# A four-layer kernel whose engine queues are ordered on another timing model

## The chip, the cores and the metric

The kernel runs on one core of a Trainium2 chip. The core has five engines that work side by side, each through its own queue, strictly in the order in which the program holds its instructions: TensorE (PE, matrix products; its weight loads are listed as PEld), VectorE (DVE), ScalarE (ACT), GpSimd (POOL) and SyncE (SP, which here only issues DMAs). An instruction that needs another engine's result waits on a semaphore, and everything behind it in its own queue waits with it.

The metric is device time in microseconds (us). Before the change the median of 3 runs is 3192.32 us (3189.55 to 3193.76).

## The reference, cut to what matters

Four batches of 1024 tokens with 128 channels go through four layers. Every layer has the same frame, with a different mixer and a different feed-forward part:

```python
xn = _layernorm(x)
s = mixer(xn)          # four kinds
g = silu(ffn(xn))      # four kinds
x = x + s * g
```

- Layer 0: a state-space mixer in chunks, and a gated feed-forward whose weights and inputs are rounded to a 4-bit grid.
- Layer 1: attention between the 16 heads of one token with 1.5-entmax (it sorts 16 scores for each head and token), and a mixture of 8 experts, of which each token uses two.
- Layer 2: a rotating linear recurrence over the tokens (16 heads, each with a 2 x 16 state), and a second mixture of experts with a shared expert.
- Layer 3: causal attention with a learned relative position term, 16 heads of 8 channels, and a gated feed-forward with 384 hidden units.

In layer 3 the part that the prediction speaks of most is

```python
srel = srel_skew(einsum('bhnd,hmd->bhnm', qx, ex))
qk = (einsum('bhnd,bhmd->bhnm', qx, kx) + srel) * inv_dim
atten = softmax(qk - mask)            # exp on ScalarE
h = silu(x @ wg.T) * (x @ wu.T)       # silu on ScalarE
```

## The kernel before, in words

The kernel is written in Python over a tile library. The code emits instructions one after another (generators are woven together by `weave`, L78 and following, so that the emitted order already mixes independent work). It doesn't say in which order an engine runs them. When the library's `TileContext` (L2228) is left, a scheduler plays the whole program through on a timing model. Whenever an engine is free in that model, it gets the earliest emitted instruction of those whose operands and buffers the model holds to be ready. The sequence that comes out is the fixed queue of each engine on the chip. So the timing model never sets a time on the chip, but it decides which instruction stands before which.

**Layer 1** works in eight units of half a batch (512 tokens). `heads1` computes a unit's head scores (products L718, sums L722), sorts them with a network of maxima and minima (`sort16`, L696 and L697, on DVE), runs two prefix scans (L750, L751) and the threshold search (L759 to L773), and forms the values (products on POOL at L788, sums on DVE at L783). `moe1` computes the router's logits (L803), ranks them (`top2`, L191 to L199), normalises the two weights (L809 to L816), splits them into three bf16 parts (`thirds`, L207 to L211) and turns these on PE (L214). Only then can the experts start: each expert scales its input (L830 on DVE), multiplies (L835 and L837 on PE), applies silu (L838 on ACT), multiplies on DVE (L839) and projects down (L826).

**Layer 2** first projects (L1100 to L1191), then computes rotation gates (`gates2`), then runs `scan2`: 8 tiles of 16 steps; a step is four dependent small DVE instructions (L1530, L1533, L1536, L1541). The steps read tables that `chunks2` makes (sums at L1396, updates at L1408 and L1409 on DVE; much of the rest on POOL). A table goes through DRAM: L1412 stores it and L1501 and L1502 load it again in the layout that the steps read. There are four tables, and tile i needs table i modulo 4. The experts of this layer (`experts2`) are emitted between the steps.

**Layer 3** handles 128 units (4 batches, 4 groups of heads, 8 query tiles), which makes 192 score tiles of up to 512 columns:

- PE computes a score tile for 4 heads (L2068) into the only `score` buffer there is (the PSUM pool `"sc"` has one buffer, so score tile x+1 waits until tile x has been compared);
- DVE scales, adds the relative term and takes the minimum (L2076, L2083);
- ACT takes the exponential (L2090), DVE transposes the result (L1797), PE multiplies it with the values (L2104);
- for later units, PE computes relative scores (L2004), ACT copies them out (L2006), DMAs store them and load them back skewed (L2009, L2010, L2025, L2031), POOL masks them (L2035).

Once per batch `ffn3` is emitted into this stream in four steps of three column blocks: PE L1953, then on ACT a silu (L1957) and a copy (L1958), a product on POOL (L1959), the down projection on PE (L1963) and another silu on ACT (L1964). ACT holds one table of functions at a time; going from exp to silu or back costs an `ACT_TABLE_LOAD`, which the compiler puts in after the order is fixed. Copies need no table of their own.

## Time and profile before

The profiled execution took 3191.88 us; its span in the profile is 3190.2 us. By stage (busy time of an engine in each stretch, in us):

| stage | from, to | length | PE | DVE | ACT | granted PE clock |
|---|---|---|---|---|---|---|
| layer 0 | 40, 578 | 538 | 401.74 | 284.90 | 270.92 | 0.87 |
| layer 1 | 578, 1278 | 700 | 513.12 | 563.95 | 244.74 | 0.80 |
| layer 2, projections | 1278, 1440 | 162 | 143.59 | 100.75 | 68.47 | 0.95 |
| layer 2, gates and scan | 1440, 2053 | 613 | 289.62 | 470.06 | 240.85 | 0.59 |
| layer 2, end | 2053, 2140 | 87 | 62.41 | 51.74 | 30.29 | 0.69 |
| layer 3 | 2140, 3190 | 1050 | 824.21 | 813.42 | 635.09 | 0.76 |

A row like `L2090 ACT ACT_TABLE_LOAD x17 | 21.8, 1283 | 0.3` is to be read as: source line, engine, operation, count; busy us, mean ns of one; idle us of the engine just before these instructions.

### The profile page before, as it was taken

To read this page: it belongs to the slowest core of one execution; us is meant where nothing else is said; L and a number is where in the kernel's file an instruction comes from. 1 tells how busy PE (TensorE), PEld (TensorE's weight loads), DVE (VectorE), ACT (ScalarE), POOL (GpSimd) and SP (SyncE) were. 2 spreads that over 40 slices of the span, in tenths; PEclk is the share of its full clock that TensorE was granted. 3 is DMA by queue.
4 is the path that set the end of the run, shared out by engine and by line. 5 is a ranking of instruction groups with operands and counts; after the bars stand their busy time and mean duration, and the time that the engine had idled before them with its cause. 6 is when DMAs were issued, how large, how long until landed. Compare 5 with 4: busy or idle time off the path is not lost. (4 is left out here: it accounts for less than half of the span.)

```text
span 3190.2 us, 50621 instructions
## 1 busy us (share of the span) xinstructions
PE 2246.5 (70%) x18321; PEld 1278.9 (40%) x18321; DVE 2302.6 (72%) x5540; ACT 1494.7 (47%) x3256; POOL 1155.6 (36%) x1086
## 2 busy tenths in 40 slices
PE   5787778577787776894443674367877877878875
PEld 2555556232333332561110222244544544545553
DVE  5555544878888886657777888656788788788786
ACT  3554544333333333525332463136665765665663
POOL 3433444144444444223477433232322322323322
PEclk9888888588878877895655566566877877877776
DMA  3000000100000000320333446328677677677772
GB/s 81 13 1 1 1 1 1 35 0 0 0 0 7 6 1 7 114 98 20 73 106 112 128 107 145 101 90 252 179 217 213 191 215 230 185 221 203 209 233 65
DMA packets 397311, 308.18 MB, mean 97 GB/s; under 512 B 96369, under 2 KB 379885, under 8 KB 391429
## 3 DMA queue, kind: packets, MB, share of 16 engines
q1 hardware_dynamic: 395908, 300.75, 32.9%
q10 hardware_dynamic: 1152, 4.19, 0.4%
q8 instruction: 144, 2.36, 0.3%
q14 instruction: 107, 0.87, 0.1%
HBM read 162.72 MB, written 141.56 MB: 95 GB/s over the span
## 5 line engine op out<-in xcount | busy, mean ns | idle before, releaser
L2090 ACT ACTIVATE neg<-neg,low 128x640 f32<-128x640 f32 (+7 forms) x512 | 390.1, 763 | 168.4 <-DVE low L2083 168.1
L2035 POOL TENSOR_SCALAR_AFFINE_SELECT rel<-rel 128x512 f32<-128x512 f32 x288 | 180.2, 637 | 625.6 <-DMA rel<-flat 459.6
L1797 DVE STREAM_TRANSPOSE wT<-neg 128x640 f32<-128x640 f32 (+7 forms) x512 | 361.7, 754 | 15.8 <-ACT neg L2090 13.4
L2068 PE MATMUL score<-k,q 32*128 32x512 f32 (+3 forms) x1536 | 276.5, 702 | 103.1 <-DVE low L2083 102.5
L2083 DVE CUSTOM_DVE_ANT_0 neg<-score,rel,low 128x128 f32<-128x128 f32 (+3 forms) x448 | 217.3, 517 | 138.2 <-issue 67.2
L2004 PE MATMUL pr<-emb,q 32*128 32x256 f32 x1024 | 227.5, 525 | 62.2 <-ACT r L2006 37.1
L2104 PE MATMUL po<-wT,vb 128*32 128x64 f32 (+1 forms) x10240 | 216.6, 241 | 44.4 <-issue 30.8
L2104 PEld LDWEIGHTS po<-wT,vb 128*32 128x32 f32 x10240 | 184.3, 128 | 144.1 <-issue 85.2
L2004 PEld LDWEIGHTS pr<-emb,q 32*128 32x128 f32 x1024 | 146.1, 249 | 136.9 <-ACT r L2006 69.1
L2006 ACT COPY r<-pr 128x512 f32<-128x512 f32 x256 | 136.4, 581 | 128.8 <-PE pr L2004 95.3
L2068 PEld LDWEIGHTS score<-k,q 32*128 32x128 f32 x1536 | 98.5, 236 | 159.8 <-DVE low L2083 115.5
L2083 DVE CUSTOM_DVE_ANT_0 neg<-score,rel 128x512 f32<-128x512 f32 (+3 forms) x320 | 149.2, 521 | 18.4 <-PE score L2068 7.2
L835 PE MATMUL pg<-xnT,w 128*128 128x512 f32 x256 | 148.1, 662 | 6.7 <-DVE h L839 3.1
L788 POOL TENSOR_TENSOR prod<-rest,kv 128x2048 f32<-128x2048 f32 x32 | 145.2, 4571 | 18.4 <-ACT rest L778 18.4
L837 PE MATMUL pu<-xin,w 128*128 128x512 f32 x256 | 141.2, 635 | 13.7 <-DVE h L839 7.6
L826 PE MATMUL po<-h,w 128*128 128x512 f32 x256 | 131.4, 635 | 26.9 <-DVE h L839 26.9
L838 ACT ACTIVATE h<-pg 128x512 f32<-128x512 f32 x128 | 75.9, 595 | 156.8 <-PE pg L835 156.7
L214 PE MATMUL pt<-ident,three 128*24 128x128 bf16 x64 | 9.2, 295 | 197.5 <-DVE three L211 197.5
L1084 PE MATMUL ph<-xin,upT 128*128 128x512 bf16 (+1 forms) x128 | 69.7, 574 | 65.2 <-DVE xin L1078 63.8
L431 PE MATMUL px<-hT,xbcT 128*128 128x512 f32 x256 | 114.7, 592 | 0.0
L1489 PE MATMUL read<-kt,const_sb 128*128 128x128 f32 x256 | 50.7, 370 | 90.3 <-POOL kt L1484 90.3
L783 DVE TENSOR_REDUCE s<-prod 128x128 f32<-128x2048 f32 x32 | 73.1, 2284 | 49.4 <-POOL prod L788 49.4
(634 smaller groups left out, 5662.8 us busy)
## 6 DMA issues: line engine op xcount, KB each, us to landing
flat<-r SPq DMA_DIRECT2D x256, 256.0 KB
rel<-flat SPq DMA_DIRECT2D x112, 512.0 KB
flat<-r SPq DMA_DIRECT2D x256, 128.0 KB
rel<-flat SPq DMA_DIRECT2D x96, 256.0 KB
kt<-kd SPq DMA_DIRECT2D x16, 512.0 KB
qt<-qd SPq DMA_DIRECT2D x16, 512.0 KB
kdc<-kdd SPq DMA_DIRECT2D x16, 512.0 KB
ktc<-ktd SPq DMA_DIRECT2D x16, 512.0 KB
```

Source lines behind the costliest of these rows:

```text
L788: nc.gpsimd.tensor_tensor(prod, attn.rearrange("p (t h g) -> p t h g", t=4, g=16)[:, t].unsqueeze(2).to_broadcast(each), kv[:, t, 1, :].re ...
L826: nc.tensor.matmul(po, W["w2"][:, e, c, :], h[:, c, :], start=(e == 0 and c == 0), stop=(e == 7 and c == 1))
L835: nc.tensor.matmul(pg, W["w1"][:, e, c * P : (c + 1) * P], xnT, start=True, stop=True)
L837: nc.tensor.matmul(pu, W["w3"][:, e, c * P : (c + 1) * P], xin, start=True, stop=True)
L1797: nc.vector.transpose(weights[at, pair][j][:, t % 2, 0 : (t + 1) * P], S[j][:, 0 : (t + 1) * P])
L2004: nc.tensor.matmul(to[:, m, :], q[at, t * P : (t + 1) * P], W["emb"][at, i, :], start=True, stop=True)
L2006: nc.scalar.copy(r[:, n], to)
L2035: nc.gpsimd.affine_select(out=rel[:, :, slot(back), :], in_=rel[:, :, slot(0), :], compare_op=op, fill=fill, base=0, pattern=[[0, 4], [-si ...
L2068: nc.tensor.matmul(sc[:, j, 0 : last - first], q[at(j), 1 + t * P : 1 + n], kk[at(j), first:last], start=True, stop=True)
L2083: nc.vector.tensor_tensor_reduce(out=neg[:, begin:last], in0=sc[:, j, begin - first : last - first], in1=rel[:, j, slot : slot + (last - b ...
L2090: nc.scalar.activation(neg[:, 0:n], neg[:, 0:n], AF.Exp, bias=here, scale=-1.0, accum_out=group["sums"][:, j, t : t + 1])
L2104: nc.tensor.matmul(o[32 * j : 32 * j + 32, 2 * pair + m.start : 2 * pair + 2, :], vb[:, kb, j].rearrange("p a d -> p (a d)"), weights[j][: ...
```

## The change

One argument is added where the library's context is opened. No instruction that computes is added, removed or resized.

```diff
     out = nc.dram_tensor("out_0", (NB, T, D), F32, kind="ExternalOutput").ap()
-    with tile.TileContext(nc) as tc:
+    with tile.TileContext(nc, schedule_with_timeline_sim=True) as tc:
         tile_kernel(tc, I, out)
```

With it, the scheduler plays the program through on the library's timeline model (engines, queues and DMAs as timelines) instead of its default model. All five queues are ordered anew, and what the compiler derives from the order (table loads, waits that need an instruction of their own) follows. On the new queues of DVE, ACT, PE, POOL and SP stand the same computing instructions as before, in another order.

## The prediction, made before the changed kernel had run

> **What bounds the kernel now.** I read the page's busy lines first, then the busy time by stage, then the waits of the two stages that are longest, and last ScalarE's timeline in layer 3. No engine is busy for more than 72% of the span, so no engine's work bounds the whole; each stage is bound by how tightly two queues mesh, and that is the one thing that this change can alter.
>
> ```profile
> span 3190.2 us, 50621 instructions
> ...
> PE 2246.5 (70%) x18321; PEld 1278.9 (40%) x18321; DVE 2302.6 (72%) x5540; ACT 1494.7 (47%) x3256; POOL 1155.6 (36%) x1086
> ```
>
> Busy time by stage (stretch, length, then PE, PEld, DVE, ACT, POOL, granted clock, DMA share, GB/s). These rows are layer 1, layer 2's projections, its gates and scan, and layer 3:
>
> ```profile
> 578.00:1278.00 700.00, 513.12 (x1156) 208.79 (x1156) 563.95 (x779) 244.74 (x459) 280.24 (x116) 0.80 0.02 6
> 1278.00:1440.00 162.00, 143.59 (x768) 99.81 (x768) 100.75 (x300) 68.47 (x145) 35.27 (x32) 0.95 0.31 104
> 1440.00:2053.00 613.00, 289.62 (x840) 117.55 (x840) 470.06 (x888) 240.85 (x476) 286.05 (x202) 0.59 0.36 93
> 2140.00:3190.00 1050.00, 824.21 (x13376) 519.27 (x13376) 813.42 (x2560) 635.09 (x1492) 304.56 (x412) 0.76 0.69 201
> ```
>
> Layer 1 and the scan are led by DVE (81% and 77% busy), layer 3 by PE and DVE together (78% and 77%). The waits of layer 1 and of layer 3 (total, times, longest):
>
> ```profile
> PE pt L214 <- DVE three L211: 108.3, 8, 16.2
> ...
> DVE s L783 <- POOL prod L788: 49.4, 28, 3.6
> ```
>
> ```profile
> ACT neg L2090 <- DVE low L2083: 168.1, 68, 8.5
> ...
> PE score L2068 <- DVE low L2083: 102.5, 88, 5.4
> ...
> DVE neg L2083 <- PE score L2068: 55.9, 47, 3.9
> ```
>
> In layer 1 PE stands idle about 13.5 us in each of 8 units until DVE has split the router's weights. In layer 3 PE and DVE take turns on the one score buffer. ScalarE's lines in layer 3, and one stretch of it inside a feed-forward:
>
> ```profile
> L2090 ACT ACT_TABLE_LOAD x17 | 21.8, 1283 | 0.3
> L1957 ACT ACT_TABLE_LOAD x9 | 11.5, 1283 | 4.4 <-issue 4.3
> ```
>
> ```profile
> 2483.86 1.28 ACT L1957 ACT_TABLE_LOAD   x1 [2.07 <-issue]
> 2485.15 0.94 ACT L1957 ACTIVATE h<-pgu 128x256 f32<-128x256 f32 x3
> 2487.88 0.92 ACT L1958 COPY up<-pgu 128x256 f32<-128x256 f32 x3 [1.79 <-DMA flat<-r]
> 2488.82 1.28 ACT L2090 ACT_TABLE_LOAD   x1
> 2490.11 1.15 ACT L2090 ACTIVATE neg<-neg,low 128x1024 f32<-128x1024 f32 x1
> ```
>
> The reader is to see that silus stand in threes between blocks of exps, so that one load serves three of them.
>
> **The change part by part.** The two orders, compared queue by queue, hold the same computing instructions. What differs, with its price:
>
> *1. Layer 3, table loads.* The new ACT order has 210 table loads instead of 169: 77 instead of 33 in layer 3, 133 instead of 136 ahead of it. The four feed-forwards hold 16, 15, 19 and 17 instead of 8, 6, 6 and 6, because exps now stand between nearly every pair of silus. That is 41 x 1.283 = 53 us of ACT, about 14 us for each of the four feed-forwards less the three loads saved elsewhere. It isn't all on the path. In the stretch from 2479 to 2533 us ACT is busy 37.64 of 54 us; with 14 more it would be at 52 of 54, so the load fills nearly all the room and any wait left over (ACT waits there 4.1 us for L1953 and 7.1 us for L1963) lengthens the stretch. Behind a load are queued exps, which DVE's transposes (L1797) wait for, and the copies of `pr` (L2006), which PE's next L2004 waits for with all scores behind it. Ends: 10 us gained (exps no longer queue behind silus that wait for PE) and 56 us lost (44 loads x 1.283, all on the path). I take half of the 53: +25.
>
> The Trainium skill, page "ScalarE: Activation LUTs", section "What ACT_TABLE_LOAD costs", gives a switch 1283 ns and a drain of about 1380 ns, 2.66 us in all. By that the 44 loads would cost 117 us of ACT. The row above shows 1283 ns and 0.3 us of idle time ahead of 17 loads together, and in the timeline the next exp starts 10 ns after the load: the drain isn't seen here, and the row decides.
>
> *2. Layer 3, who stands between the scores.* Score tile x+1 waits for the compare of x, so a tile's cycle is at least the longer of (score on PE, other DVE work before the next compare) plus the longer of (compare on DVE, other PE work before the next score). From rows: a 512-wide score takes 2.13 us for its eight matmuls, a compare 0.70 us a head plus 0.08 to read its minimum, a 1024-wide transpose 1.22, a value product 216.6 us / 5120 = 0.042, a relative product 227.5 / 512 = 0.44. Summed over the 192 tiles in the two orders, that is 1150 us before and 1193 after: the new order sets work less evenly. The trace took 1007 us from the first compare to the last, so the arithmetic overstates by 1.14; the 43 us become at most 38. DVE's transposes stand a little nearer to their exps as well (2.8 instead of 3.1 compares between). Ends: 15 gained (the unevenness may fall into the 56 us that DVE waits for scores anyhow) and 38 lost; as the sum ignores all slack, I take a third of it, +13.
>
> *3. Layer 1.* In seven of the eight units DVE's router chain (L191 to L211) stands 24 to 43 places earlier, between the L839 products of the unit before, and the sort is spread between those products too. PE's 108.3 us of waiting for L211 go. What is late next: from a unit's last L839 to the next unit's first L837 the trace has 850.5 to 884.3, 33.7 us, with DVE busy 28.66 of the 34. In the new order DVE has in the same place three value sums (2.29 each), two products and two sums of scores (2.28 each), two scans (2.28 each) and about 8 us of sort and copies: 29 us, all ahead of the first L830. So the wait moves from L214 to L837, which waits for L830, and the gap shrinks from 34 to about 31. In the dense part (797 to 850: PE 47.75, DVE 43.26 of 53) there are up to 4 us to gain, but DVE's 2.3 us instructions now stand in front of the L839 that PE waits for. Ends: 15 lost (2 a unit) and 50 gained (6 to 7 a unit). I take 3 for each of seven units: -20.
>
> *4. Scan.* Two things get worse. A table's last update now stands 12, 17, 14 and 22 DVE instructions ahead of the tile that reads it, instead of 27, 103, 142 and 118. Between lie the store and the load: in the trace the store of table 0 is issued at 1631.87, its loads at 1636.03 to 1638.4, so some 4 us a leg and 10 us in all; the few instructions between (about 8 to 10 us by their rows) cover most of it, leaving 0 to 5 us at each of three tiles. And 402 instead of 360 scan instructions follow another scan instruction directly; those start about 0.05 us after it, while behind other work they start 0.08 us before its end: 42 x 0.13 = 5 us. What gets better: 18 us in which DVE waits for POOL's L1393 products now have scan steps to fill them. Ends: 15 gained, 25 lost; I take +8.
>
> *5. Projections.* PE is busy 143.59 of 162 us and dense after the first 10.8 us, so a new order has little to give: 5 gained to 10 lost, taken as +2.
>
> *6. Layers 0 and 2's end, SP, POOL.* Most of layer 0's ACT instructions (227 of 328) keep their place, and its other queues move by 1 to 4 places: 0, with 6 us either way. On SP, layer 3's stores (L2009, L2010) stand 2.5 places later, its loads of q and k (L1975) 6 earlier and of v (L1985) 18 earlier; SP issues in order, so the stores stand behind loads whose buffers may not be free. The cover is that a relative tile is loaded three units ahead, about 23 us at 62 us for 8 units; without it DVE's L2083 would wait, as it now does for no more than 3.8 us at a time. POOL's selects move by 1 to 8 places and POOL is 29% busy there. Both 0. DVE gets 79 more waits that stand as instructions of their own, about 17 ns each in the trace: 1 us.
>
> Sum: +25 +13 -20 +8 +2 = +28. Against the profiled execution's 3191.88 us (0.4 us under the median 3192.32) that makes 3220.
>
> **The rivals.**
>
> *Layer 1 wins the day (faster).* DVE is idle for 136 us in layer 1, because value sums wait for POOL (49.4 us) and scans and thresholds for POOL and ACT; the new order puts sort instructions in just those places. If half of the idle time closes, layer 1 falls by 68 us, and the sum is 3192 - 68 + 48 = 3172. It decides from 48 us on, 6 a unit. For it: the places are the right ones. Against it: the stretch between units holds as much DVE work as before.
>
> *ACT takes layer 3 over.* All loads and all unevenness land on the path: +56 +38 -20 +10 = +84, 3276. For it: ACT would have 2 us of room in a 54 us stretch. Against it: outside the feed-forwards ACT is only 58% to 68% busy, so it catches up.
>
> *Nothing that can be told.* The runs lie within 0.13% of each other; 0.2%, 6 us, is what a measurement can tell. Gains and losses of 20 to 50 us that cancel to 6 give 3186 to 3198. That the change did nothing at all is excluded, since the queues differ.
>
> **How the numbers follow.** My forecast (3200 to 3245) 0.48, layer 1 wins 0.26, ACT takes over 0.16, cancelling 0.10. The range goes from 3155, below the first rival's 3172, to 3276, the second's; what lies outside are bounds that would all have to fall on one side. The likeliest case's own range is 3200 to 3245. Chances: faster 0.28 (the first rival and a little of the cancelling), same 0.09, slower 0.63.
>
> **What would show it.** Right: ACT_TABLE_LOAD at 77 in layer 3 with the feed-forward groups of units longer by some 6 us (they now take 69 to 72 us for 8 units, the others 52 to 67); L214's wait gone and L837 waiting for L830 in its place; first steps of tiles 1 to 3 waiting for a DMA. Wrong: layer 1 under 646 us, or layer 3 not longer than 1050.

## The result, and the profile after

The changed kernel takes 3315.36 us (median; 3300.26 to 3317.26), the kernel before 3193.04 us beside it. The ratio is 1.0374, with a 95% interval from 1.0342 to 1.0406: slower by 122 us. The forecast was 3220 us and the range ended at 3276, so the direction was right; the time lies 95 us above the forecast and 39 above the range's end.

The head of the page, and the engines' busy time:

```profile
span 3315.6 us, 50740 instructions
...
PE 2313.4 (70%) x18321; PEld 1312.7 (40%) x18321; DVE 2418.4 (73%) x5540; ACT 1550.0 (47%) x3297; POOL 1178.6 (36%) x1086
```

Busy time by stage in the changed kernel (stretch, length, then PE, PEld, DVE, ACT, POOL, granted clock, DMA share, GB/s). The rows are: start, layer 0, layer 1, layer 2's projections, its gates and scan, its end, layer 3.

```profile
0.00:64.00 64.00, 12.98 (x35) 6.04 (x35) 33.07 (x151) 9.45 (x21) 21.15 (x38) 1.00 0.29 66
64.00:604.00 540.00, 405.73 (x1906) 293.45 (x1906) 282.37 (x736) 263.20 (x614) 204.29 (x260) 0.84 0.03 9
604.00:1306.00 702.00, 529.05 (x1156) 211.28 (x1156) 649.13 (x772) 244.22 (x459) 292.98 (x116) 0.80 0.02 5
1306.00:1463.00 157.00, 139.73 (x768) 98.67 (x768) 97.09 (x304) 66.15 (x143) 33.33 (x32) 0.94 0.32 108
1463.00:2042.00 579.00, 293.04 (x840) 120.66 (x840) 475.01 (x889) 240.87 (x477) 296.59 (x203) 0.59 0.39 98
2042.00:2136.00 94.00, 64.23 (x240) 40.30 (x240) 56.02 (x132) 31.07 (x52) 27.33 (x27) 0.68 0.33 119
2136.00:3315.60 1179.60, 868.69 (x13376) 542.26 (x13376) 825.67 (x2560) 695.04 (x1536) 302.89 (x411) 0.74 0.62 178
```

Against the lengths before, the stages moved like this (us):

| stage | before | after | change | predicted |
|---|---|---|---|---|
| start | 40 | 64 | +24 | not in the sum |
| layer 0 | 538 | 540 | +2 | 0 |
| layer 1 | 700 | 702 | +2 | -20 |
| layer 2, projections | 162 | 157 | -5 | +2 |
| layer 2, gates and scan | 613 | 579 | -34 | +8 |
| layer 2, end | 87 | 94 | +7 | 0 |
| layer 3 | 1050 | 1179.6 | +130 | +38 |

Two things stand out. Layer 1 kept its length although VectorE's busy time there rose from 563.95 to 649.13 us for the same instructions. And layer 3 lost more than three times what was forecast. Its waits after the change (total, times, longest):

```profile
...
PE score L2068 <- DVE low L2083: 217.8, 105, 9.8
...
DVE neg L2083 <- PE score L2068: 98.0, 51, 12.2
...
DVE neg L2083 <- POOL rel L2035: 28.7, 7, 12.2
...
DVE ln_st L136 <- DMA x<-x: 25.5, 3, 8.7
```

The lockstep of TensorE and VectorE has come apart on both sides: 217.8 instead of 102.5 us of TensorE's waiting, 98.0 instead of 55.9 of VectorE's. VectorE's waits for relative tiles that GpSimd has still to mask (L2035) have grown from 8.8 us to 28.7. The last line is new. ScalarE's table loads in layer 3 after the change (busy us, mean ns of one, idle before):

```profile
L2090 ACT ACT_TABLE_LOAD x39 | 50.0, 1283 | 0.7
L1957 ACT ACT_TABLE_LOAD x22 | 28.2, 1283 | 6.1 <-PE pgu L1953 5.3 <-DMA k<-qk 0.5
...
L1964 ACT ACT_TABLE_LOAD x13 | 16.7, 1283 | 0.2
```

With three more at L138 these are the 77 loads that the order said there would be.

Layer 3 runs in 16 groups of 8 units. The time from a group's first compare (L2083) to the next group's, read from the trace, shows where the loss lies. Groups 1, 5, 9 and 13 hold the feed-forwards; groups 2, 6 and 10 hold the layernorm and projections of the next batch (`begin3`).

| group | 0 | 1 | 2 | 3 | 4 | 5 | 6 | 7 | 8 | 9 | 10 | 11 | 12 | 13 | 14 | 15 | sum |
|---|---|---|---|---|---|---|---|---|---|---|---|---|---|---|---|---|---|
| before | 63.5 | 72.5 | 60.2 | 64.4 | 61.6 | 69.6 | 60.6 | 58.4 | 60.3 | 71.1 | 60.4 | 60.7 | 62.4 | 68.9 | 56.9 | 51.6 | 1003.1 |
| after | 69.9 | 76.1 | 74.4 | 61.4 | 61.3 | 84.6 | 79.0 | 59.6 | 68.6 | 84.4 | 74.8 | 60.8 | 63.2 | 96.8 | 59.7 | 55.5 | 1130.0 |

Of 127 us, 60 lie in the feed-forward groups, 47 in the three `begin3` groups, 20 in the other nine.

### The profile page after: what moved, and what is told of

The parts are those of the page before. It is cut to its first block, busy times and chain, and to the rows that moved or that the text cites. A ratio compares the mean times of both kernels' runs of the same rounds, so it can differ in the third digit from the quotient of the medians.

```text
span 3315.6 us, 50740 instructions
## 1 busy us (share of the span) xinstructions
PE 2313.4 (70%) x18321; PEld 1312.7 (40%) x18321; DVE 2418.4 (73%) x5540; ACT 1550.0 (47%) x3297; POOL 1178.6 (36%) x1086
## 5 line engine op out<-in xcount | busy, mean ns | idle before, releaser
L2035 POOL TENSOR_SCALAR_AFFINE_SELECT rel<-rel 128x512 f32<-128x512 f32 x288 | 179.7, 635 | 739.5 <-DMA rel<-flat 512.6
L2068 PE MATMUL score<-k,q 32*128 32x512 f32 (+3 forms) x1536 | 264.5, 713 | 218.1 <-DVE low L2083 217.8
L1797 DVE STREAM_TRANSPOSE wT<-neg 128x640 f32<-128x640 f32 (+7 forms) x512 | 367.0, 758 | 64.4 <-ACT neg L2090 59.4
L2083 DVE CUSTOM_DVE_ANT_0 neg<-score,rel,low 128x128 f32<-128x128 f32 (+3 forms) x448 | 218.0, 519 | 109.2 <-PE score L2068 86.1
L2104 PEld LDWEIGHTS po<-wT,vb 128*32 128x32 f32 x10240 | 195.1, 129 | 182.5 <-issue 115.0
L2004 PE MATMUL pr<-emb,q 32*128 32x256 f32 x1024 | 237.7, 526 | 38.4 <-ACT up L1958 12.3
L2104 PE MATMUL po<-wT,vb 128*32 128x64 f32 (+1 forms) x10240 | 245.5, 245 | 26.1 <-DVE wT L1797 17.2
L2083 DVE CUSTOM_DVE_ANT_0 neg<-score,rel 128x512 f32<-128x512 f32 (+3 forms) x320 | 149.1, 521 | 83.0 <-ACT r L2006 35.1
L2006 ACT COPY r<-pr 128x512 f32<-128x512 f32 x256 | 137.7, 581 | 153.7 <-PE pr L2004 89.3
L2068 PEld LDWEIGHTS score<-k,q 32*128 32x128 f32 x1536 | 91.8, 240 | 270.3 <-DVE low L2083 190.6
L2004 PEld LDWEIGHTS pr<-emb,q 32*128 32x128 f32 x1024 | 153.6, 248 | 92.2 <-issue 28.5
L788 POOL TENSOR_TENSOR prod<-rest,kv 128x2048 f32<-128x2048 f32 x32 | 151.2, 4744 | 74.8 <-DVE s L783 50.2
L835 PE MATMUL pg<-xnT,w 128*128 128x512 f32 x256 | 151.7, 677 | 32.4 <-DVE h L839 15.0
L826 PE MATMUL po<-h,w 128*128 128x512 f32 x256 | 144.3, 653 | 31.9 <-DVE h L839 31.9
L837 PE MATMUL pu<-xin,w 128*128 128x512 f32 x256 | 145.6, 653 | 25.2 <-DVE h L839 12.9
L838 ACT ACTIVATE h<-pg 128x512 f32<-128x512 f32 x128 | 76.1, 595 | 171.9 <-PE pg L835 171.6
L2076 DVE TENSOR_SCALAR_CACHE_REDUCE neg<-score 128x384 f32<-128x384 f32 (+2 forms) x192 | 80.4, 419 | 50.0 <-PE score L2068 50.0
L839 DVE TENSOR_TENSOR h<-h,pu 128x512 f32<-128x512 f32 x128 | 86.3, 677 | 17.5 <-ACT h L838 9.7
L214 PE MATMUL pt<-ident,three 128*24 128x128 bf16 x64 | 9.2, 295 | 124.3 <-DVE three L211 123.1
```

Of the source, the lines that this page charges most:

```text
L788: nc.gpsimd.tensor_tensor(prod, attn.rearrange("p (t h g) -> p t h g", t=4, g=16)[:, t].unsqueeze(2).to_broadcast(each), kv[:, t, 1, :].re ...
L826: nc.tensor.matmul(po, W["w2"][:, e, c, :], h[:, c, :], start=(e == 0 and c == 0), stop=(e == 7 and c == 1))
L835: nc.tensor.matmul(pg, W["w1"][:, e, c * P : (c + 1) * P], xnT, start=True, stop=True)
L837: nc.tensor.matmul(pu, W["w3"][:, e, c * P : (c + 1) * P], xin, start=True, stop=True)
L1797: nc.vector.transpose(weights[at, pair][j][:, t % 2, 0 : (t + 1) * P], S[j][:, 0 : (t + 1) * P])
L2004: nc.tensor.matmul(to[:, m, :], q[at, t * P : (t + 1) * P], W["emb"][at, i, :], start=True, stop=True)
```

## The experiments

All variants but one use the same means. A first build, never launched, gives the order that a model makes. A second build gets edges between neighbours of one queue that fix that order (an edge sets only which instruction stands first; it adds no wait). So any stage's queues, or a single queue of a stage, can be taken from either model. Queues that no edge holds are planned anew by the timeline model around those that are held.

```diff
+def follow(order, keep):
+    def pin(tc, traced, stage):
+        at, last = {ins.name: ins for ins in traced}, {}
+        for name in order:
+            ins = at.get(name)
+            if ins is None or not keep(ins, stage.get(name)):
+                continue
+            if ins.engine in last:
+                tc.add_manual_dep(ins, last[ins.engine].name, NoSync, reason="order")
+            last[ins.engine] = ins
+    return pin
```

`default` and `timeline` below are the two models' orders; stage 0 is the preparation, 1 to 4 are layer 0 to layer 3. "Layer 3" in the tables is the sum of the 16 groups above (1003.1 before, 1130.0 after).

### Which stage, and a better kernel

```diff
+follow(default, lambda ins, stage: stage == 4)      # l3_default
+follow(timeline, lambda ins, stage: stage != 4)
```

> Layer 3's five queues stand in the default model's order, all other stages in the timeline model's. If layer 3's loss lies in its own order: layer 3 back from 1180 us to 1045 to 1060, the whole at 3180 to 3200, what stays being the longer start (+22), paid by the scan (-34). If the loss was handed over by the stages before it (clock, late loads): layer 3 at 1090 or more, the whole above 3225.

Measured: 3187.53 us, ratio to the kernel before 0.998 (0.9969 to 0.9991); layer 3 at 1004.6. The whole loss of layer 3, 128 us by the medians (3315.36 - 3187.53), is in layer 3's own order. Nothing was handed over by the stages ahead of it.

```diff
+follow(timeline, lambda ins, stage: stage == 3)     # l2_timeline
+follow(default, lambda ins, stage: stage != 3)
```

> Only layer 2's queues stand in the timeline model's order, all other stages in the default model's. If the scan's gain is its own: layer 2 (862 us before, 830 after the change) at 825 to 835 and the whole at 3155 to 3168, faster than both kernels. If the gain was lent by the stages beside it: layer 2 at 850 or more, the whole at 3180 or more.

Measured: 3157.21 us, ratio 0.9881 (0.9865 to 0.9898). This version beats both kernels. Layer 2's projections, scan and end are as long as in the changed kernel within 1 us (156, 578 and 94 us instead of 157, 579 and 94). The scan's row:

```profile
1434.00:2012.00 578.00, 288.98 (x840) 119.25 (x840) 473.43 (x893) 242.60 (x478) 296.53 (x203) 0.60 0.40 99
```

Why the scan gains is read from VectorE's waits in the two traces; no run tests it by itself. Before, in gates and scan:

```profile
DVE A L1396 <- POOL gram L1393: 25.0, 17, 5.2
...
DVE kt L1481 <- POOL kt L1478: 11.6, 5, 4.0
DVE KT L1381 <- POOL pre L1358: 8.0, 1, 8.0
...
DVE kt L1481 <- POOL kt L1472: 6.9, 1, 6.9
```

After, in the same stage:

```profile
DVE prod L1530 <- DMA ktc<-ktd: 9.9, 3, 5.0
DVE A L1397 <- POOL F L1376: 5.5, 1, 5.5
...
DVE kt L1481 <- POOL kt L1478: 4.0, 1, 4.0
```

The waits for GpSimd fall by 25.0 + 11.6 + 6.9 + 8.0 - 5.5 - 4.0 = 42 us; three first steps wait for their tables, 9.9 us in all. The net is 32, of the stage's 34.

### Table loads

```diff
-                nc.scalar.activation(h[:, c, :], pgu[:, 0, :], AF.Silu)
+                nc.scalar.copy(h[:, c, :], pgu[:, 0, :])
...
-            nc.scalar.activation(g[:, half, first : first + 2], po, AF.Silu)
+            nc.scalar.copy(g[:, half, first : first + 2], po)
```

Once with all queues in the timeline order, once with all in the default order:

> All queues in the changed kernel's order, but both silus of layer 3's feed-forward (L1957, L1964) are left out: a copy of the same size stands in their place, which needs no table. 70 of layer 3's 77 table loads go, 90 us of ScalarE. Theory 'table loads' (they are what layer 3 lost): layer 3 falls from 1180 us by 55 to 90, the whole to 3225 to 3260. Theory 'order' (instructions that cannot start yet stand ahead of others that could): layer 3 falls by no more than the 44 added loads' half, 10 to 30, the whole at 3285 to 3305.

> The same two silus left out in the kernel before, its queues in their own order. 26 of 33 table loads go, 33 us of ScalarE. Both theories: layer 3 falls from 1050 us by 5 to 25, the whole to 3167 to 3187. The difference to the same edit in the changed order is what the added loads cost.

Measured: 3263.2 us (ratio 1.0216, 1.0185 to 1.0246) in the changed order, 3191.99 us (0.9991, 0.9978 to 1.0004) in the order before. In both, 7 loads are left in layer 3. The loads cost 52 us of the changed kernel by the medians, and nothing that can be told in the kernel before, where I had expected 5 to 25: there taking out 26 loads, 33 us of ScalarE, gained 7 us at the most by the interval. (A copy takes 368 ns where the silu at L1957 took 387, which is 1 us over all of them.) The changed kernel's value, 52, lies between what the two theories had named (55 to 90, and 10 to 30); layer 3's sum falls from 1130.0 to 1081.2, so more than half of the loss has another cause. The feed-forward groups fall from 76.1, 84.6, 84.4 and 96.8 to 67.9, 77.0, 77.3 and 77.1; the `begin3` groups do not fall as a set (78.8, 75.7, 73.7).

### The layernorm that stands ahead of its data

VectorE in the changed kernel, in group 2 (start, length, engine, line; in brackets the idle time before and what ended it):

```profile
2323.50 0.48 DVE L2083 CUSTOM_DVE_ANT_0 neg<-score,rel,low 128x256 f32<-128x256 f32 x1
2323.91 0.08 DVE L2083 DVE_READ_ACCUMULATOR2_ANT low<- 128x1 f32 x1
2332.32 0.87 DVE L136 BATCH_NORM_STATS2 ln_st<-x 128x6 f32<-128x128 f32 x4 [8.33 <-DMA x<-x]
2333.11 0.36 DVE L137 BATCH_NORM_AGGREGATE ln_mv<-ln_st 128x2 f32<-128x6 f32 x4
2333.39 0.58 DVE L2083 CUSTOM_DVE_ANT_0 neg<-score,rel,low 128x384 f32<-128x384 f32 x1
```

VectorE stands still for 8.33 us until the next batch's input has landed, and the next score's compares, which don't need it, stand behind it. In the kernel before the same statistics stand some ten compares later and wait for nothing:

```profile
2328.01 0.29 DVE L136 BATCH_NORM_STATS2 ln_st<-x 128x6 f32<-128x128 f32 x1
```

The edit moves them back to that place, and the timeline model plans the rest of layer 3 around it:

```diff
+for names in begins:                                 # the three begin3
+    norm = [name for name in names if at[name].engine == DVE]
+    for name in norm:                                # ln_late: only norm[0]
+        tc.add_manual_dep(at[name], tenth_later_compare, NoSync, reason="later")
```

> As the changed kernel, but in layer 3 each of the three begin3 layernorms starts ten compares (L2083) later on VectorE, behind 122 instead of 112 in its batch, as in the kernel before; the timeline model plans the rest of layer 3 around that, all other stages keep the changed order. Theory 'layernorm ahead of its data' (VectorE stands 8.5 us three times for a load with compares behind it): the three waits of together 25.5 us go, and some of the late exps behind them; the groups of units 2, 6 and 10 (74, 79 and 75 us) fall to 60 to 68 each, layer 3 by 25 to 45, the whole to 3270 to 3290. Rival (VectorE would only wait for scores instead): 10 us or less.

Measured: 3288.6 us (ratio 1.0293, 1.0273 to 1.0314), groups 2, 6 and 10 at 68.7, 69.3 and 69.4. The edge held only one of eight statistics, so VectorE still stood 25.4 us for the loads; what changed is the rest of the chain, which ended later. In group 2 of the changed kernel ScalarE loads the square root's table at 2338.73, normalises, and reaches the next exp at 2346.79, and VectorE's transposes wait 4.79 us for it. In this run four exps of the same width stand ahead of that table load (at 2339.21 to 2340.70, the load at 2341.31), and the transposes do not wait. So the 27 us by which the time fell are not owed to the wait I had named, which is as long as it was. That they are owed to this part is read from this one group; the rest of layer 3 was planned anew as well.

> As the run ln_late, but all of a layernorm's VectorE instructions (eight L136, eight L137, L139, L141) of the three begin3s stand behind the tenth later compare, where in ln_late only one L136 of eight did and VectorE still stood 25.4 us for the loads. Theory 'layernorm ahead of its data': the wait DVE ln_st L136 <- DMA goes, the groups of units 2, 6 and 10 fall from 74, 79 and 75 us to 60 to 66, layer 3 by 35 to 50 against the changed kernel, the whole to 3262 to 3280. Rival (the wait only changes its name, scores or relative tiles being late as well): those groups stay at 68 to 70 as in ln_late, the whole at 3285 or more.

Measured: 3284.44 us (1.028, 1.0246 to 1.0315), layer 3 at 1101.2, the three groups at 70.6, 69.7 and 68.2. The wait for the load is gone from VectorE's list, but its waits for scores are as long as in the changed kernel (99.5 instead of 98.0 for L2083) and the groups are still 8 to 10 us longer than before. So the rival's outcome came: putting the whole early layernorm back (with the rest of layer 3 planned around it, 75 table loads instead of 77) gains 31 us, and the wait of 25.5 us that I had taken for its core is worth no more than the difference of the two runs, 4 us, which their intervals don't tell from nothing.

> The queues of the run ln_all_late, with both silus of layer 3's feed-forward left out as in nosilu_after (copies in their place, no table needed). If the added loads (52 us, nosilu_after) and the early layernorm (31 us, ln_all_late) are separate causes, they add up: the whole at 3225 to 3238. If both only uncover the same slack: 3250 or more.

Measured: 3234.35 us (1.0114, 1.0038 to 1.0189), layer 3 at 1043.8. Loads and layernorm add up: 52 + 31 = 83 expected, 3315.36 - 3234.35 = 81 measured. What is left of layer 3's loss is 1043.8 - 1003.1 = 41 us: 25 in the three `begin3` groups (68.9, 67.9 and 69.7, still 7 to 9 us each above the kernel before), 5 in the feed-forward groups and 10 in the other nine.

### One queue, or how they mesh

```diff
+follow(default, lambda ins, stage: stage == 4 and ins.engine.name in ("Activation",))
+follow(timeline, lambda ins, stage: stage != 4)
```

with the engines of each run's name; the timeline model plans layer 3's other queues around them, so that no run changes one queue alone.

> As the changed kernel, but ScalarE's queue of layer 3 stands in the default model's order (33 table loads there instead of 77); the timeline model plans the other four queues of layer 3 around it. If the loads alone are the price of ScalarE's order: layer 3 falls from 1180 us by 45 to 60 as with the silus left out, the whole to 3255 to 3270. If ScalarE's order sets the others' too: by 100 to 130, 3185 to 3215. If loads cost nothing in themselves: by less than 20.

> As the changed kernel, but TensorE's queue of layer 3 stands in the default model's order; the timeline model plans the other four queues of layer 3 around it (65 or fewer loads result, 49 in layer 3). After the run l3_act (ScalarE alone in the default order, no gain) two ways are open. If TensorE's order leads the others: layer 3 falls from 1180 us by 70 to 120. If no single queue does, and only all five together mesh: by less than 40.

> As the changed kernel, but VectorE's queue of layer 3 stands in the default model's order, the timeline model plans the other four around it. If VectorE's order (scores, transposes, layernorm) is what loses the 45 us that loads and layernorm leave open: layer 3 falls by 60 to 90, the whole to 3225 to 3255. If no single queue carries it: by 20 to 45 for its layernorm alone, 3270 to 3295.

> As the changed kernel, with ScalarE's and TensorE's queues of layer 3 both in the default model's order (33 loads there), VectorE's, GpSimd's and SyncE's planned around them by the timeline model. One alone gave 0 (ScalarE) and 25 us (TensorE). If the loss is that queues no longer mesh, two that fit together give more than the sum of both: 60 to 110, the whole at 3205 to 3255. If it is a sum of single costs: 20 to 35, at 3280 or more.

> As the changed kernel, with TensorE's and VectorE's queues of layer 3 in the default model's order, ScalarE's (49 loads there), GpSimd's and SyncE's planned around them. These two take turns on the one score buffer. If their meshing carries the loss: layer 3 falls by 90 to 125, the whole at 3190 to 3225, although ScalarE keeps 16 added loads. If ScalarE's order carries it: by less than 50.

| layer 3's queues in the default order | loads in layer 3 | layer 3 | whole | ratio (95%) |
|---|---|---|---|---|
| none (the changed kernel) | 77 | 1130.0 | 3315.36 | 1.0374 (1.0342 to 1.0406) |
| ScalarE | 33 | 1130.5 | 3316.9 | 1.0376 (1.0356 to 1.0397) |
| TensorE | 49 | 1105.6 | 3290.34 | 1.0309 (1.027 to 1.0348) |
| VectorE | 71 | 1105.7 | 3291.31 | 1.0292 (1.0219 to 1.0364) |
| ScalarE, TensorE | 33 | 1094.8 | 3279.92 | 1.0256 (1.0187 to 1.0325) |
| TensorE, VectorE | 49 | 1048.8 | 3230.42 | 1.0101 (1.003 to 1.0173) |
| all five | 33 | 1004.6 | 3187.53 | 0.998 (0.9969 to 0.9991) |

Restoring ScalarE's order alone takes 44 loads away and gains nothing. That is the third of the cases named, but not for its reason, since the loads do cost 52 us where they stand: the feed-forward groups stay long (86.3, 79.2, 80.7, 79.3, together 16 us under the changed kernel), the `begin3` groups are together 16 us shorter, and the other nine 32 us longer. ScalarE now waits for products that TensorE makes later (L2006 for L2004: 144.1 us instead of 89.3, L1964 for L1963: 59.8 instead of 14.6, L1957 for L1953: 57.8 instead of 19.5). VectorE's 24 us are a net sum too: its feed-forward and `begin3` groups are 70 us shorter, the other nine 45 longer. TensorE and VectorE together give 81 us of layer 3, more than their single 24 and 24, though less than the 90 to 125 that I had named: outside the feed-forward groups and group 0 all groups are back within 2.5 us of the kernel before. TensorE's wait for the score buffer there, and in the run without silus and with the late layernorm (line numbers shifted by an insertion):

```profile
PE score L2068 <- DVE low L2083: 116.5, 90, 8.3
```

```profile
PE score L2091 <- DVE low L2106: 171.9, 101, 6.6
```

It is 102.5 before, 217.8 after, 171.9 when loads and layernorm are dealt with, 116.5 when both queues have the old order. That the 41 us that remain are this lockstep is not shown: no run takes it away and leaves loads and layernorm as they are, and the readings speak against it as the whole of them. TensorE's wait doesn't follow the length of layer 3: it is 171.9 us where the layer takes 1043.8, and 116.5 where it takes 1048.8. VectorE's waits for scores at L2083 are 108.2 us with both queues in the old order, more than the changed kernel's 98.0, although layer 3 is 81 us shorter there; and 25 of the 41 us lie in the three `begin3` groups. In the run without silus and with the late layernorm VectorE also waits 27.5 us for relative tiles (8.8 before) and 30.9 for exps at L1797 (13.4 before). A lower granted TensorE clock isn't what remains: it is 0.77 in layer 3 of that run, 0.76 before. In the changed kernel it is 0.74, and TensorE's same instructions take 868.69 instead of 824.21 us; no run separates what part of the loss that is.

### The start

ScalarE, then VectorE, in the changed kernel's first 40 us:

```profile
38.10 0.31 ACT L615 ACTIVATE bias<-bias 128x128 f32<-128x128 f32 x1 [18.34 <-DMA bias<-in_L_attn_bq]
38.32 0.28 ACT L138 ACTIVATE ln_rs<-ln_mv,eps 128x4 f32<-128x4 f32 x1
```

```profile
23.80 0.67 DVE L136 BATCH_NORM_STATS2 ln_st<-x_all 128x6 f32<-128x128 f32 x3
38.63 0.18 DVE L139 RECIPROCAL ln_rs<-ln_rs 128x4 f32<-128x4 f32 x1 [14.16 <-ACT ln_rs L138]
```

Layer 1's bias (L615) waits for its load until 38.1 us, layer 0's L138 stands behind it on ScalarE, VectorE's L139 waits for L138, and the rounding of layer 0's weights stands behind L139. The kernel before has the same wait at L615, but there the rounding of these weights (L163 to L177, 19.5 to 33.0 us) stands ahead of L139:

```profile
38.59 0.31 ACT L615 ACTIVATE bias<-bias 128x128 f32<-128x128 f32 x1 [12.16 <-DMA bias<-in_L_attn_bq]
```

```profile
40.54 0.18 DVE L139 RECIPROCAL ln_rs<-ln_rs 128x4 f32<-128x4 f32 x1 [6.30 <-ACT ln_rs L138]
```

```diff
+follow(timeline, lambda ins, stage: ins.name != bias)
+tc.add_manual_dep(at[bias], layer0_on_ScalarE[99], NoSync, reason="later")
```

> As the changed kernel, with one instruction moved: ScalarE's scaling of layer 1's bias (L615), which waits for its load until 38.1 us, stands 100 places of layer 0's work later. Everything else keeps the changed order. Theory (VectorE's L139 waits 14.2 us for ScalarE's L138, which stands behind L615, and the rounding of layer 0's weights stands behind L139): that wait goes and layer 0 begins at 42 to 50 us instead of 64, the whole at 3293 to 3302. Rival (the start is long because layernorm work itself stands ahead of the rounding on VectorE): layer 0 begins at 58 or later, the whole above 3308.

Measured: 3305.18 us (1.0345, 1.0324 to 1.0367), span 3303.5 against 3315.6. Layer 0 begins at 49.4 us instead of 63.8 (42.2 before), and L138 runs at once:

```profile
21.15 0.30 ACT L138 ACTIVATE ln_rs<-ln_mv,eps 128x4 f32<-128x4 f32 x1 [1.53 <-DVE ln_mv L137]
```

One instruction of 0.31 us in the wrong place is worth 14 of the 22 us by which layer 0 begins later. The whole falls by 10 us (medians) or 12 (spans), less than the 13 to 22 that I had named, and the two intervals overlap, so the whole times alone don't show it. The other 7 look like the layernorm work that VectorE does ahead of the rounding; that wasn't tried.

### Layer 1: the sort beside the products

Two rows of VectorE in layer 1, before and after (busy us, mean ns of one, idle before):

```profile
L696 DVE TENSOR_TENSOR sorted<-sorted 128x512 f32<-128x512 f32 x24 | 18.5, 773 | 0.3
L697 DVE TENSOR_TENSOR sorted<-sorted 128x512 f32<-128x512 f32 x24 | 18.5, 770 | 0.0
```

```profile
L696 DVE TENSOR_TENSOR sorted<-sorted 128x512 f32<-128x512 f32 x24 | 40.9, 1706 | 0.4
L697 DVE TENSOR_TENSOR sorted<-sorted 128x512 f32<-128x512 f32 x24 | 29.2, 1216 | 0.0
```

The sort as a whole (L696, L697) takes 184 instead of 118 us; a few small instructions such as L141 (9.5 instead of 1.2 us) add the rest of the 85. By the trace's start and end times, the L696s and L697s that overlap no GpSimd instruction take 0.50 to 0.52 us in either kernel (a mean over all widths); those that do overlap one take 2.05 and 1.84 us on average in the changed kernel, mostly beside L788, and there are 59 of them instead of 17. To see the pair by itself:

```diff
+for beside, work in ((0, sort), (1, None), (1, sort), (1, reduce), (1, gate)):
+    begin()
+    if beside:
+        products()          # 4 on GpSimd, 128x2048, as L788
+    if work:
+        work()              # on VectorE
```

> Computes nothing of the task (the output is zeros). Five stretches one after another: 24 maxima of 128x512 on VectorE alone (both inputs in SBUF, as the sort's); 4 products of 128x2048 on GpSimd alone (as L788); the maxima beside the products; 8 sums of 128x2048 (one SBUF input, as L783) beside the products; 24 products with one PSUM input (as L839) beside the products. Theory 'they cannot run side by side' (layer 1's sort took 1706 ns instead of 773 in the changed order): a maximum alone takes 0.6 to 0.8 us, beside a product several us; sums stay at 2.28 and PSUM products at 0.68. Rival 'the sort was long for another reason' (its own waits, ScalarE's copies): the maxima beside the products take what they take alone.

The timeline of that run (start, length; one row is all instructions of a stretch):

```profile
13.59 14.47 DVE L37 TENSOR_TENSOR b<-a 128x512 f32<-128x512 f32 x24
...
45.23 17.78 POOL L30 TENSOR_TENSOR prod<-attn,kv 128x2048 f32<-128x2048 f32 x4 [44.79 <-DVE kv L26]
...
65.60 31.60 DVE L37 TENSOR_TENSOR b<-a 128x512 f32<-128x512 f32 x24
65.76 19.45 POOL L30 TENSOR_TENSOR prod<-attn,kv 128x2048 f32<-128x2048 f32 x4 [2.75 <-DVE kv L26]
...
110.05 18.48 DVE L41 TENSOR_REDUCE small<-wide 128x128 f32<-128x2048 f32 x8
110.21 17.78 POOL L30 TENSOR_TENSOR prod<-attn,kv 128x2048 f32<-128x2048 f32 x4 [25.00 <-DVE kv L26]
...
141.26 14.37 DVE L45 TENSOR_TENSOR b<-a,pu 128x512 f32<-128x512 f32 x24
141.42 17.84 POOL L30 TENSOR_TENSOR prod<-attn,kv 128x2048 f32<-128x2048 f32 x4 [13.43 <-DVE kv L26]
```

Alone, 24 maxima take 14.47 us and four products 17.78. Side by side they take 31.60, nearly the sum (32.25): one at a time. Four of these maxima last 4.96 us, one for each product of 4.8 to 4.9 us; the other 20 take 0.63 to 0.68. Sums with one SBUF input and products with one PSUM input show no such loss beside GpSimd (18.48 / 8 = 2.31 us against 2.28 for L783 in the kernel, and 14.37 / 24 = 0.60 us, as a maximum alone), nor do the four products beside them (17.78 and 17.84).

Then in place:

```diff
-        nc.gpsimd.tensor_tensor(prod, ..., ALU.mult)
+        nc.gpsimd.memset(prod, 1.0)
```

> All queues in the changed kernel's order, but in layer 1 GpSimd writes a constant into the 128x2048 tile (a fill, which reads nothing) instead of multiplying (L788); the attention values of layer 1 are left out by that. Theory 'the sort cannot run beside a product that reads SBUF': L696 and L697 of 128x512 fall from 1706 and 1216 ns to 770 to 800, VectorE's busy time in layer 1 from 649 us to 560 to 580, layer 1 from 702 us by 40 to 80. Rival (the sort is long for another reason): their means stay above 1100 ns.

> The same fill in the kernel before, its queues in their own order. The sort stands apart from the products there (773 and 770 ns), so nothing is gained on it: VectorE's busy time stays at 560 to 565; what can go is VectorE's wait for the products (49.4 us) as far as the fill is shorter than the 4.57 us product. Layer 1 falls from 700 us by 0 to 50. If the changed order is the better one in layer 1 but for the contention, fill_after's layer 1 is shorter than this one by 15 to 50.

Layer 1 in the changed order, then in the order before:

```profile
598.50:1215.00 616.50, 512.53 (x1156) 207.51 (x1156) 569.17 (x795) 245.78 (x460) 198.64 (x116) 0.83 0.03 8
```

```profile
576.00:1209.00 633.00, 479.54 (x1156) 197.52 (x1156) 550.71 (x799) 245.60 (x459) 192.12 (x116) 0.84 0.03 8
```

Whole times: 3226.84 us (1.0097, 1.0068 to 1.0125) and 3119.85 us (0.9767, 0.974 to 0.9795). In the changed order L696 and L697 fall to 870 and 683 ns (I had said 770 to 800) and VectorE's busy time to 569.17; layer 1 falls by 85.5 us, a little more than the 40 to 80 I had said. In the order before, VectorE's busy time falls as well, by 13 us to 550.71, where I had said 560 to 565: there, too, sort steps had stood beside the products (those that read `score` take 11.0 us instead of 24.1). A fill takes 1.81 us instead of a product's 4.7, so part of what both runs gain is GpSimd's shorter time; in the kernel before, that and those 13 us together are 67 us (700 to 633), more than the 50 that I had set as its most. The comparison of the two fills holds the fill's length the same: without L788's reads on GpSimd the new order of layer 1 is 16.5 us shorter than the old one (one profile of each).

## Why the prediction was wrong, point by point

The step that failed most is the price of layer 3, +38 in the sum and +128 by the runs: loads at 52 us instead of 25, early layernorms at 31 instead of nothing, and 45 left where 13 had been put for the scores. Beside it the start stood at nothing and cost 24, and layer 1's gain of 20 didn't come. Point by point:

- **Layer 3, table loads** (+25, ends -10 and +56): mechanism right, size off. The term measures 52 us, nearly its upper end. "I take half of the 53" failed: the working's own 52 busy of 54 us of ScalarE already said that there was no room, and the discount had no row behind it. The Trainium skill's price for a switch with its drain ("ScalarE: Activation LUTs", "What ACT_TABLE_LOAD costs", 2.66 us) would give, as an estimate, 186 us of ScalarE for the 70 loads that were taken away. The 52 us of the whole that were measured don't decide between page and row, since a part of ScalarE's time may be slack; the changed kernel's rows do, with 1283 ns a load again and 0.7 us of idle time ahead of 39 of them together.
- **Layer 3, between the scores** (+13, ends -15 and +38): too small by some 30 us if all that is left of layer 3 without loads and layernorm, 41 us, belongs to it, and that is not shown. The sum over 192 tiles, 1150 to 1193, gave 43 us; that the two agree so closely may be chance. "As the sum ignores all slack, I take a third of it" had no row behind it. One of the sum's prices was misread as well: 2.13 us for a 512-wide score is what it takes at a granted clock of 0.5. In the trace before, of the 76 such scores whose eight matmuls stand together, 40 took 1.13 to 1.14 us, at a clock of 1.0, and 29 took 2.0 to 2.2, at 0.50 to 0.58.
- **Layer 3, what was not in the sum:** the layernorms of `begin3`, 31 us. The working followed table loads and scores on ScalarE, TensorE and VectorE, but not where the instructions stand that wait for a load from DRAM. In the order they were ten compares ahead of their old place. Item 6 put the relative tiles at 0 under the cover of three units; VectorE's waits for them went from 8.8 us, longest 3.8, to 28.7, longest 12.2. What that costs wasn't tried.
- **The "What would show it" signs** held for layer 3 (77 loads; feed-forward groups longer), but those groups grew by 4, 15, 13 and 28 us, not by some 6. Neither sign of being wrong came up (layer 1 at 702, layer 3 at 1180): they asked for a layer 3 that was too short, not for one that was too long.
- **Layer 1** (-20): the step as told came true. L214's wait fell from 108.3 to 21.7 us, VectorE's waits for GpSimd's products from 49.4 to 7.9, and with the contention out of the way the order is worth 16.5. What failed is the durations: I priced the moved sort at the duration of its row, where it stood alone, and 85 us of VectorE's time came on top. Before the change, then after it:

```profile
PE po L826 <- DVE h L839: 26.9, 11, 3.8
```

```profile
PE po L826 <- DVE h L839: 31.9, 11, 8.1
PE pt L214 <- DVE three L211: 21.7, 1, 21.7
PE pg L835 <- DVE h L839: 15.0, 11, 4.4
...
PE pg L835 <- DVE xin L830: 11.7, 3, 6.3
```

```profile
DVE s L783 <- POOL prod L788: 7.9, 5, 2.2
```

  The wait moved in part to L830, as told (L835 and L837 wait 19.2 us for it instead of 4.4), and in a larger part to L839 (L826, L835 and L837 wait 59.8 us for it instead of 37.6). The working had named the 2.3 us instructions in front of L839 as a possible loss; with the fill, which leaves the order as it is, these waits are 19.9 us, so those instructions are not the whole of it. The Trainium skill has a rule that spoke against this step and that I did not weigh ("SBUF — State Buffer", "Who interferes with whom"): a VectorE instruction with two SBUF inputs contends with a GpSimd instruction that reads SBUF, for a pair of ports that only one of them can hold at a time, while a VectorE reduction never contends. The run with the pair by itself agrees on both counts (31.60 us for 14.47 and 17.78; 2.31 us a sum beside products).
- **Scan** (+8): wrong in sign. The loss was sized well (0 to 5 us at each of three tiles; measured 9.9 in three waits, longest 5.0). The gain was not: I counted 18 us of waits for GpSimd's L1393 products, of which at most 15 could fill, and waits for GpSimd of 42 us went. The row for L1396 alone shows 25.0, and those for L1481 and L1381 were there to be added up.
- **The start** was named nowhere and cost 24 us by the stretches (40 to 64). "Layers 0 ...: most instructions keep their place" counted places moved by layer and missed that on VectorE a wait that goes back to a load (L139, for L138 behind L615) changed places with the rounding.
- **Projections** (+2): -5. **Layer 2's end** (0): +7, in the run with layer 2 alone as well; its cause wasn't tried.
- **The rivals:** none decided. The nearest, ScalarE taking layer 3 over (3276), had the loads right (56 against 52 us) and the rest of layer 3 too small (38 against 76). "Layer 1 wins the day" failed on the durations.

The sum that the runs support: +52 +31 +45 (loads, layernorm, and what is left of the 128, by the medians) +24 +2 +2 -5 -34 +7 = +124, against 122 measured. Against the prediction's terms nearly all of it is a miss to the slow side (loads 27, scores at most 32, layernorms 31, start 24, layer 1 22); that the whole missed by no more than 95 is luck, as the scan's term missed by 42 to the other.

## What to carry to other kernels

When an order changes, look first at every instruction that waits for a load from DRAM or for a chain that does, and at what now stands behind it on its queue: one 0.31 us copy cost 14 us of the start and three layernorms 31 of the whole, though not by the wait for the load itself. Price a moved instruction for its new neighbours, not by its old row: whether it still runs at that speed depends on what the other engine does at that time. And judge an order stage by stage: the same change was worth -34 us in the scan and +128 in layer 3, and taking only the good part gave 3157 us.

## What the runs showed of the hardware

- VectorE maxima with both inputs in SBUF and GpSimd products that read SBUF run one at a time: 31.60 us together for 14.47 and 17.78, four maxima of 4.96 us among 20 of 0.63 to 0.68. Reductions (2.31 us) and instructions with one PSUM input (0.60 us) run beside them unhindered. In layer 1 VectorE's idle time fell from 136 to 53 us and its busy time rose by 85: what looked like room was filled with the same instructions, made longer.
- A table load has no fixed worth. 26 loads taken out of the old order were worth nothing that could be told (0.9991, 0.9978 to 1.0004), 70 out of the new one 52 us, and 44 taken out by restoring ScalarE's queue alone again nothing (3316.9 against 3315.36 us), with the other queues planned anew around it.
- Within layer 3 the time of a score goes with the granted clock: eight matmuls of a 512-wide score took 1.14 us at 1.0 and 2.09 at 0.5. The profile models the ends of matmuls; from the first start to the eighth, medians of 40 and 29 scores, it was 0.55 and 1.03 us.
